# Row scatters of a group's last block: all at once, or two by two between other pieces of work

## The chip, the cores and the metric

The kernel runs on one core of one Trainium2 chip. The metric is the time of one execution on the device in microseconds (us). The core has five engines with an instruction queue each, and each queue runs in order: TensorE (PE, matrix products; PEld is its loading of weights), VectorE (DVE), ScalarE (ACT), GpSimd (POOL) and SyncE (SP, which issues most DMAs here). An engine waits for another one, or for a DMA, by a semaphore.

## The reference, cut to what matters

The input is x, 8 sequences of 1024 rows of 256 numbers, all in f32. An RWKV layer (a time mix with a scan along the sequence, then a channel mix with a hidden width of 1024) is followed by a layer of 32 routed experts, of which every row uses four. The change lies in how rows reach the experts.

```python
x = x + rwkv(layernorm(x))          # time mix, then channel mix
xn = layernorm(x)                   # 8192 rows of 256
gates = sigmoid(xn @ expert_sel.T)  # 32 experts
sel_val, sel_idx = top_k(gates, 4)
...
scores = relu(einsum('nd,edf->nef', xn, keys)) * gate_full[:, :, None]
out = x + einsum('nef,efv->nv', scores, values)   # 128 hidden units each
```

## The kernel before, in words

**Blocks and periods.** The rows are cut into 16 blocks of 512, two to a sequence. The main loop runs `period(i)` for i = 0 to 16. A period works on three blocks at once, by hand-written order: the channel mix of block i (`channel`, TensorE's products at L244 and L423), the time mix of block i + 1 (`mix_wk`, `mix_vr`, `mix_scan`, `mix_out`, `norm_c`), and the norm and routing of block i - 1 (`norm_d`, `apply_d`, `turn_d`, `gates_of`, `rows_of`, `scatter`). Between these pieces stand 15 calls of `advance()`. When a block's channel mix is over, its residual goes to DRAM (`acc<-x`, L445, on SyncE's queue); in the profile these stores mark the ends of the periods.

**Scatters.** Routing copies each row four times, to the regions of its experts in a DRAM buffer `xs` of its group. One scatter is an indirect DMA on GpSimd (L563), which sends 128 rows to 128 places; a block has 4 x 4 = 16. `scatter(i)` does not issue them: it puts 16 entries on the list `waiting`. `post(count)` issues the first `count` of the list, and `behind_others` keeps a scatter behind the GpSimd work that stands ahead of it in the program. GpSimd's other work in a period is the residual add of `norm_c` (L371, 2.4 us) and, in every second period, four copies of the scan's last column (`tail`, L320 and L321). The rows to scatter lie in a tile `x3` that has two buffers, so `apply_d` of block i + 2 (ScalarE, L363) writes where block i's rows were.

**Expert groups.** The blocks form two groups, `GROUPS = ((12, 6, 1.8, 4, 0.8), (4, 4, 1.0, 2, 1.0))`: blocks 0 to 11 and blocks 12 to 15. The numbers behind the size are: advances to wait before the table is made, tiles per advance, a pause, and sums per advance. A group's rows are worked in tiles of 256 rows of one expert (112 tiles for group 0, of which the last 16 are made of two halves with an expert each; 48 for group 1). `expert_group` is a stream that runs in the background: it makes the table that says which expert and which rows each tile has (`tile_table`, some 45 small steps on VectorE with three matrix products), then the tiles (`experts`), then the sums of the four results of each row (`combine`). A tile is fetched from `xs` on SyncE (L759), transposed on TensorE (`trx`, L794), multiplied by its expert's keys (`ph`, L806), passed through ScalarE (`hs`, L884), multiplied by the values (`po`, L822), copied by ScalarE (`yg`, L888) and scattered by GpSimd in two indirect DMAs to `ys` (L834). The three products of a tile lie two steps apart: in step n TensorE does `po` of tile n - 4, `ph` of tile n - 2 and `trx` of tile n. For group 0 the stream rests four resumptions between the first fetches and step 0 (the first `pause`).

**advance.** Each call issues one waiting scatter and lets each background stream do the work that its pace allows: a `yield` of 1.0 takes one advance, a `yield` of 1.8 a part of 1 / 1.8.

**Around the change.** Group 0's stream begins ahead of period 13 (`i == groups[g][-1] + 2`), group 1's after period 16; both times, `post(len(waiting))` first issues all waiting scatters. After that, `drain()` calls `advance()` until the streams are done. `blocks_over` then gives the tiles more buffers: `yg` takes turns with a tile of the channel mix, and fetches run five tiles ahead and not three. `x` and `out` are not touched by the change, nor is the number of any instruction that computes.

Of the kernel before, what the change touches and what calls it, by code (L numbers as in the profile page):

```python
# [34 lines left out]
def rwkv_then_routed_experts(  # L35
# [48 lines left out]
    group_of = {i: g for g, members in enumerate(groups) for i in members}  # L84
# [34 lines left out]
    def load_experts(part):  # L119
        es = slice(part * NE // 4, (part + 1) * NE // 4)  # L120
        tc.keep_in_program_order(nc.sync.dma_start(out=wexp[:, es], in_=w_exp[:, es]))
# [44 lines left out]
    def apart(kind, g, ins):  # L166

        key = f"{kind}_{g}"
        tc.declare_no_dep(ins.ins, group=key, reason="the rows are disjoint")
        tc.add_to_no_dep_group(key, ins.ins)  # L170

    def clear(g):


        zeros = p2.tile([P, DX], F32, tag="g", name=f"zeros_{g}")
        nc.gpsimd.memset(zeros, 0.0)
        nc.gpsimd.memset(zeros[:, D : D + 1], NOWHERE)
        front_rows = xs[g][: regions[g], :].rearrange("(e r) d -> e r d", e=NE)[:, :TS, :]
        fills = []
        for j in range(SJ):  # L180
            fills.append(
                nc.sync.dma_start(
                    out=front_rows[:, j * P : (j + 1) * P, :].rearrange("e p d -> p e d"),
                    in_=zeros[:, None, :].to_broadcast([P, NE, DX]),
                )
            )
            fills.append(
                nc.sync.dma_start(
                    out=xs[g][regions[g] + j * P : regions[g] + (j + 1) * P, :], in_=zeros
                )  # L190
            )
        for fill in fills:
            apart("scatter", g, fill)
# [345 lines left out]
    waiting = []  # L539
# [5 lines left out]
    def behind_others(s):  # L545

        own_names.add(s.ins.name)
        for other in reversed(nc.cur_bb.bb.instructions):
            if other.engine == ET.Pool and other.name not in own_names:
                tc.add_manual_dep(  # L550
                    s.ins,
                    other.name,
                    mybir.DependencyInfo(mybir.DependencyClass.NoSync, mybir.DependencyReason.DATA),
                    reason="the norms go first",
                )
                return

    def post(count):

        for i, t, k in waiting[:count]:  # L560
            m = mine[i]
            g = group_of[i]
            s = nc.gpsimd.indirect_dma_start(  # L563
                out=xs[g],
                out_offset=bass.IndirectOffsetOnAxis(ap=m["row"][:, t, k : k + 1], axis=0),
                in_=m["x3"][:, t, :],
                in_offset=None,
            )
            apart("scatter", g, s)
            behind_others(s)  # L570
        del waiting[:count]
# [381 lines left out]

    def advance():

        post(1)
        for entry in list(background):
            entry[1] += 1.0
            while entry[1] > 0.0:
                try:  # L960
                    entry[1] -= 1.0 / next(entry[0])
                except StopIteration:
                    background.remove(entry)
                    break

    def drain():
        while background:
            advance()

    def beside(stream):  # L970
        next(stream)
        background.append([stream, 0.0])
# [5 lines left out]
    def period(i):  # L978


        do(norm_d, i - 1)
        if i:
            do(mix_wk, i + 1, 0)
        advance()
        do(turn_c, i)
        if i:
            do(mix_vr, i + 1, 0)
        advance()
        do(apply_d, i - 1)
        do(fetch_block, i + 2)  # L990
        do(receptance, i)
        advance()
        do(channel, i, 0)
        if i:
            do(mix_scan, i + 1, 0)
        advance()
        if i:
            do(mix_wk, i + 1, 1)
        do(turn_d, i - 1)
        do(norm_a, i + 2)  # L1000
        advance()
        do(channel, i, 1)
        advance()
        if i:
            do(mix_vr, i + 1, 1)
        advance()
        do(channel, i, 2)
        do(mix_scan, i + 1, 1)
        advance()
        do(gates_of, i - 1)  # L1010
        do(channel, i, 3)
        do(norm_b, i + 2)
        advance()
        do(channel, i, 4)
        advance()
        do(mix_out, i + 1)
        do(norm_c, i + 1)
        advance()
        do(channel, i, 5)
        do(rows_of, i - 1)  # L1020
        do(scatter, i - 1)
        do(turn_b, i + 2)
        advance()
        do(channel, i, 6)
        advance()
        do(channel, i, 7)
        do(gates_by_row, i - 1)
        advance()
        do(apply_c, i + 1)
        do(channel_end, i)  # L1030
        advance()
# [21 lines left out]
    apply_c(0)  # L1053
    mix_scan(1, 0)

    done = set()

    def expert_group(g, wait, tiles, pause, sums):

        making = tile_table(g)  # L1060
        next(making)
        for _ in range(wait):
            yield 1.0
        for _ in making:
            pass

        while g and ("tiles", g - 1) not in done:
            yield 1.0
        for _ in experts(g, 0 if g else 4):
            yield tiles  # L1070
        done.add(("tiles", g))
        for _ in range(pause):
            yield 1.0
        while g and ("sums", g - 1) not in done:
            yield 1.0
        for _ in combine(g):
            yield sums
        done.add(("sums", g))

    for i in range(total_blocks + 1):  # L1080
        for g, (size, *pace) in enumerate(GROUPS):
            if i == groups[g][-1] + 2:
                post(len(waiting))
                beside(expert_group(g, *pace))
        period(i)
        if i + 1 < len(groups):
            clear(i + 1)
        elif 2 <= i < 6:
            load_experts(i - 2)
    blocks_over.append(True)  # L1090
    post(len(waiting))
    beside(expert_group(len(groups) - 1, *GROUPS[-1][1:]))
    drain()

# [44 lines left out]
```

## Time and profile before

| | us |
|---|---|
| median of 9 runs | 1501.15 (1497.11 to 1504.19) |
| the profiled execution | 1500.02 |
| its span in the profile | 1498.2 |
| granted TensorE clock, mean | 0.928 |
| GpSimd's row scatters (L563) | 256 of them, 255.1 busy |
| GpSimd's scatters of results (L834) | 320 of them, 320.3 busy |
| TensorE busy | 1278.1, 85% of the span |

In the lines shown further on, a line of a timeline gives the start (us from the span's beginning), the duration, the engine, the line of the kernel, the operation, what it writes and reads, its shape, how many such instructions are merged in the line, and in brackets how long the engine had been idle before it and what ended that. "remote" there means that no engine's instruction in the profile fits the moment of the release; "issue" means that the engine waited for nothing that the profile shows. A group's line ends with its busy time, the mean of one instruction in ns, and the idle time ahead of it. In the rows of 40 digits each digit is a slice of 37.5 us, in tenths of busy time.

### The profile page before, as it was taken

To read this page: it belongs to the slowest core of one execution; us is meant where nothing else is said; L and a number is where in the kernel's file an instruction comes from. 1 tells how busy PE (TensorE), PEld (TensorE's weight loads), DVE (VectorE), ACT (ScalarE), POOL (GpSimd) and SP (SyncE) were. 2 spreads that over 40 slices of the span, in tenths; PEclk is the share of its full clock that TensorE was granted. 3 is DMA by queue.
4 is the path that set the end of the run, shared out by engine and by line. 5 is a ranking of instruction groups with operands and counts; after the bars stand their busy time and mean duration, and the time that the engine had idled before them with its cause. 6 is when DMAs were issued, how large, how long until landed. Compare 5 with 4: busy or idle time off the path is not lost. (4 is left out here: it accounts for less than half of the span.)

```text
span 1498.2 us, 18501 instructions
## 1 busy us (share of the span) xinstructions
PE 1278.1 (85%) x5332; PEld 908.7 (61%) x5332; DVE 973.5 (65%) x3058; ACT 552.4 (37%) x1058; POOL 639.6 (43%) x643
## 2 busy tenths in 40 slices
PE   6999999999999998998958999998977748887720
PEld 2566667665665665665635767776765637666620
DVE  6777887886786786776837566543444524465697
ACT  3444444444444444443423343342322202434310
POOL 2003145134134134135070565665666665665640
PEclk9999999999999999999979999999988869989965
DMA  9901133133022021022031354454454543699898
GB/s 324 294 29 36 44 128 110 51 128 131 16 75 71 20 76 69 18 70 78 14 115 51 125 178 139 143 178 140 146 184 142 165 149 94 219 347 358 296 325 324
DMA packets 119412, 209.73 MB, mean 140 GB/s; under 512 B 17130, under 2 KB 77574, under 8 KB 118800
## 3 DMA queue, kind: packets, MB, share of 16 engines
q1 hardware_dynamic: 89616, 138.71, 29.0%
q0 software_dynamic: 27648, 68.23, 12.4%
q10 hardware_dynamic: 2048, 1.61, 0.3%
q8 instruction: 44, 0.72, 0.2%
q14 instruction: 56, 0.46, 0.1%
HBM read 105.68 MB, written 111.17 MB: 145 GB/s over the span
## 5 line engine op out<-in xcount | busy, mean ns | idle before, releaser
L834 POOL DMA_INDIRECT ys<-yg,to x320 | 320.3, 1001 | 226.1 <-ACT yg L888 116.9
L563 POOL DMA_INDIRECT xs<-x,row x256 | 255.1, 997 | 83.0 <-issue 67.1
L244 PE MATMUL pj_f<-xT,wkey 128*128 128x512 f32 x512 | 244.5, 600 | 1.7 <-ACT hs L884 1.2
L423 PE MATMUL cm<-wval,k 128*128 128x256 f32 x1024 | 240.9, 380 | 0.1
L822 PE MATMUL po<-wexp,hs 128*128 x640 | 185.3, 416 | 64.9 <-ACT hs L884 54.1
L423 PEld LDWEIGHTS cm<-wval,k 128*128 128x128 f32 x1024 | 194.8, 191 | 74.8 <-issue 50.1
L806 PE MATMUL ph<-xgT,key 128*128 128x256 f32 (+1 forms) x768 | 182.6, 371 | 23.2 <-DVE key L785 8.9
L878 DVE COPY xgT<-trx 128x512 f32<-128x512 f32 x112 | 77.0, 687 | 184.1 <-PE trx L794 70.8
L371 POOL TENSOR_TENSOR x<-x,xa 128x1024 f32<-128x1024 f32 x16 | 37.7, 2357 | 328.9 <-issue 317.2
L822 PEld LDWEIGHTS po<-wexp,hs 128*128 128x128 f32 x640 | 121.3, 208 | 87.9 <-ACT hs L884 59.3
L806 PEld LDWEIGHTS ph<-xgT,key 128*128 128x128 f32 x768 | 141.1, 208 | 47.6 <-DVE key L785 11.5
L884 ACT ACTIVATE hs<-ph 128x256 f32<-128x256 f32 x160 | 62.2, 389 | 283.5 <-PE trx L794 115.4
L415 ACT ACTIVATE k<-pj_f 128x512 f32<-128x512 f32 x128 | 76.5, 598 | 187.2 <-PE pj_f L244 179.4
L244 PEld LDWEIGHTS pj_f<-xT,wkey 128*128 128x128 f32 x512 | 93.3, 192 | 73.1 <-issue 67.7
L917 DVE SCALAR_TENSOR_TENSOR ac<-g,gate,ac 128x256 f32<-128x256 f32 x256 | 120.9, 484 | 22.2 <-DMA g<-ys 14.4
L794 PE MATMUL trx<-ident,xg 128*128 128x128 f32 x640 | 103.1, 287 | 12.2 <-ACT hs L884 9.1
L325 DVE RECIPROCAL rw<-rw 128x512 f32<-128x512 f32 x32 | 107.3, 3352 | 1.0
L794 PEld LDWEIGHTS trx<-ident,xg 128*128 128x128 f32 x640 | 84.6, 150 | 29.8 <-ACT hs L884 10.0
L785 DVE COPY key<-wexp 128x256 f32 x192 | 57.7, 308 | 58.6 <-remote 20.7
L888 ACT COPY yg<-po 128x512 f32<-128x512 f32 x160 | 93.8, 587 | 1.5 <-PE po L822 1.5
L321 POOL COPY tail<-ek 128x1 f32<-128x1 f32 x16 | 16.6, 1040 | 163.3 <-DVE ek L317 139.8
L397 PE MATMUL rec<-att,xT 128*128 128x256 f32 x256 | 71.5, 439 | 17.2 <-ACT xT L383 9.9
(162 smaller groups left out, 1764.6 us busy)
## 6 DMA issues: line engine op xcount, KB each, us to landing
xg<-xs SPq DMA_DIRECT2D x128, 264.0 KB
g<-ys SPq DMA_DIRECT2D x64, 512.0 KB
xs<-zeros SPq DMA_DIRECT2D x4, 4224.0 KB
xg<-xs SPq DMA_DIRECT2D x64, 132.0 KB
x<-in_x SPq DMA_DIRECT2D x16, 512.0 KB
acc<-x SPq DMA_DIRECT2D x16, 512.0 KB
wexp<-in_w_exp SPq DMA_DIRECT2D x4, 2048.0 KB
ac<-acc SPq DMA_DIRECT2D x16, 512.0 KB
```

The source lines that it names most:

```text
L244: nc.tensor.matmul(ps, w(c), rhs[:, c, :], start=(c == 0), stop=(c == KC - 1))
L325: inverse = nc.vector.reciprocal(rc, rc)
L415: nc.scalar.activation(k2, ps, AF.Relu)
L423: nc.tensor.matmul(m["cm"][t // 2][:, t % 2, :], k2[:, t * P : (t + 1) * P], wval[:, f, :], start=(f == 0 and t % 2 == 0), stop=(f == FC - 1),
L563: s = nc.gpsimd.indirect_dma_start(out=xs[g], out_offset=bass.IndirectOffsetOnAxis(ap=m["row"][:, t, k : k + 1], axis=0), in_=m["x3"][:, t ...
L794: nc.tensor.transpose(ps[:, c, j * P : (j + 1) * P], xg[:, j, c * P : (c + 1) * P], ident)
L806: nc.tensor.matmul(ps[:, cols], key[:, c * P : (c + 1) * P], xgT[:, c, cols], start=(c == 0), stop=(c == KC - 1),)
L822: nc.tensor.matmul(ps[:, j, :], hs[:, j * P : (j + 1) * P], wexp[:, bass.ds(e, 1), KC * P :], start=True, stop=True,)
L834: s = nc.gpsimd.indirect_dma_start(out=ys[g], out_offset=bass.IndirectOffsetOnAxis(ap=to[:, j : j + 1], axis=0), in_=yg[:, j, :], in_offse ...
L878: after(move(xgT, trx), signal)
L888: after(nc.scalar.copy(yg, po), signal)
L917: nc.vector.scalar_tensor_tensor(ac, gk, routed[i][:, t, k : k + 1], ac, ALU.mult, ALU.add)
```

## The change

`advance` issues two scatters where the first waiting one is of a group whose stream has begun, else one as before. The two calls of `post(len(waiting))` are gone, so the scatters that wait when a stream begins are issued two by two by the following advances. The stream makes its table as before, and then yields, an advance at a time, until none of its group's scatters waits; only then come its fetches and tiles.

```diff
     def advance():
 
-        post(1)
+        post(2 if waiting and group_of[waiting[0][0]] in begun else 1)
         for entry in list(background):
...
-    done = set()
+    done, begun = set(), set()
 
     def expert_group(g, wait, tiles, pause, sums):
 
+        begun.add(g)
         making = tile_table(g)
         next(making)
         for _ in range(wait):
             yield 1.0
         for _ in making:
             pass
+
+        while any(group_of[i] == g for i, _, _ in waiting):
+            yield 1.0
 
         while g and ("tiles", g - 1) not in done:
             yield 1.0
@@
     for i in range(total_blocks + 1):
         for g, (size, *pace) in enumerate(GROUPS):
             if i == groups[g][-1] + 2:
-                post(len(waiting))
                 beside(expert_group(g, *pace))
         period(i)
...
     blocks_over.append(True)
-    post(len(waiting))
     beside(expert_group(len(groups) - 1, *GROUPS[-1][1:]))
     drain()
```

## The prediction

> **What bounds the kernel now.** I read the page first, for the span and the slices; then the busy time by stage, cut where a block's residual is stored (SyncE's `acc<-x` at 645.82, 699.44, 761.48, 863.96, 980.56 and 1092.89 us); then GpSimd's and the other engines' timelines at the two places that the change touches.
>
> From the page:
>
> ```profile
> span 1498.2 us, 18501 instructions
> PE   6999999999999998998958999998977748887720
> POOL 2003145134134134135070565665666665665640
> L834 POOL DMA_INDIRECT ys<-yg,to x320 | 320.3, 1001 | 226.1 <-ACT yg L888 116.9
> L563 POOL DMA_INDIRECT xs<-x,row x256 | 255.1, 997 | 83.0 <-issue 67.1
> ```
>
> From its second slice to slice 28 TensorE is at 8 or 9 tenths but for one hole, slice 20 (749 to 787 us), just where GpSimd is busiest; later it is the less busy one. A scatter takes 1.0 us, and 1.27 from start to start.
>
> Stage by stage (length, busy time and instructions of each engine, granted clock, DMA):
>
> ```profile
> core 0: us, PE busy (x) PEld busy (x) DVE busy (x) ACT busy (x) POOL busy (x), PEclk, DMA share, GB/s
> 645.80:699.40 53.60, 53.11 (x206) 34.77 (x206) 42.23 (x124) 23.82 (x43) 20.84 (x22) 1.00 0.17 58
> 699.40:761.50 62.10, 56.62 (x209) 36.08 (x209) 42.81 (x131) 24.61 (x44) 18.02 (x17) 0.95 0.15 53
> 761.50:864.00 102.50, 82.74 (x344) 58.68 (x343) 57.18 (x223) 32.71 (x62) 42.92 (x43) 0.88 0.31 98
> 864.00:980.60 116.60, 113.59 (x533) 87.18 (x532) 72.15 (x234) 44.44 (x93) 74.41 (x73) 1.00 0.48 154
> 980.60:1092.90 112.30, 102.74 (x477) 81.08 (x477) 47.84 (x198) 39.52 (x85) 67.44 (x69) 0.94 0.49 152
> 1092.90:1201.70 108.80, 80.40 (x368) 64.64 (x366) 49.89 (x221) 26.51 (x62) 71.24 (x72) 0.86 0.53 168
> 1201.70:1230.30 28.60, 8.59 (x26) 6.45 (x27) 4.60 (x23) 1.96 (x6) 18.35 (x19) 0.62 0.40 134
> 1230.30:1289.40 59.10, 48.10 (x280) 42.45 (x279) 27.14 (x115) 17.12 (x40) 37.63 (x38) 0.90 0.36 106
> ```
>
> The rows are periods 11 to 16, then the drain up to group 0's last send. Period 11 is a block alone: 53.6 us, all TensorE. Period 14 holds a block and 28 tiles and is all TensorE: (116.6 - 53.6) / 28 = 2.25 us a tile. In the last row 19 tiles (38 sends) take 59.1 us, 3.11 each, with GpSimd issuing 1.28 us apart for 82% of it. Two rows do little: period 13, and the 28.6 us at 1201.7, with 8.6 us of TensorE.
>
> Period 13's start, on GpSimd:
>
> ```profile
> 746.04 2.35 POOL L371 TENSOR_TENSOR x<-x,xa 128x1024 f32<-128x1024 f32 x1 [39.51 <-issue]
> 748.55 0.99 POOL L563 DMA_INDIRECT xs<-x,row  x1 [0.15 <-issue]
> ...
> 783.20 0.96 POOL L563 DMA_INDIRECT xs<-x,row  x1 [0.30 <-issue]
> 791.01 1.10 POOL L321 COPY tail<-ek 128x1 f32<-128x1 f32 x1 [6.85 <-DVE rs_d L230]
> ```
>
> and on TensorE and ScalarE:
>
> ```profile
> 761.61 1.04 PE L237 MATMUL tr_c<-ident,xn 128*128 128x128 f32 x8
> 772.69 0.78 ACT L383 ACTIVATE xT<-tr_c,csb 128x512 f32<-128x512 f32 x1 [10.65 <-remote]
> 782.52 0.78 ACT L383 ACTIVATE xT<-tr_c,csb 128x512 f32<-128x512 f32 x1 [9.06 <-remote]
> ```
>
> The 23 held scatters and the 5 before them make one unbroken run of 28, 748.5 to 784.2. TensorE's transposes are over at 762.7, yet ScalarE copies them out only at 772.69 and 782.52, and "remote" says that no engine's work released it then. VectorE's table steps, 0.2 us each, stand one to two us apart. It ends as the run ends. Shorter cases agree: the run of 15 that ends at 706.5 holds ScalarE's same copy 7.1 us, in period 12 (62.1 us, 8.5 over period 11); period 11, whose runs are 8 at most, has no such wait. So I read a long run of scatters as delaying the signals between the other engines while it lasts.
>
> **The change, part by part.** A period has 15 calls of advance and a block 16 scatters, so the backlog grows by one a period: 23 wait when period 13 begins (7 of block 10, 16 of block 11), 15 when the drain begins.
>
> *1. Period 13 loses its stall.* In the built program's order GpSimd now has 11 scatters behind norm_c's add (748.5 to about 762.5, at 1.27), then two, six, two and four between the tail copies, then the add of block 14 and eight more. This is period 11's pattern (8, tail, 2, tail, 2) with longer runs. Of the 102.5 us, 53.6 is the block, about 22.5 ten tiles at 2.25, about 4.5 the front ends of four more (four transposes at 0.60, two products at 1.03, from the timeline); 21.9 is stall. At least none of it goes, at most all; I keep 3 for the runs of six and eight, since period 11's run of 8 cost nothing to see and period 12's run of 15 cost 8.5. Gain 18.9.
>
> *2. The tiles start later.* The table is still made at the sixth advance; the fetches now follow the twelfth. Four resumptions are pause, 1.8 go to an advance: before, 18 resumptions give 14 steps in period 13; now 8 give 4. In the built order ten fewer tiles are sent before the drain as well. Ten tiles leave a period where each costs 2.25 (gain 22.5) and join the drain, where each costs 3.11 (loss 31.1): net loss 8.6. Bounds of the drain's price: 2.25 if GpSimd kept out of the way, 3.89 at period 16's pace (108.8 / 28, its own 16 scatters in it); 3.11 is the row of the same stage. Periods 14 to 16 keep 27 steps each.
>
> *3. What the new wait holds.* The fetch waits on SyncE for group 0's last scatter. Period 11's add starts 39.2 us in (685.04), so here near 801 to 803; 2.4 us for it, three scatters (3.8), then landing: first fetch near 809, against 808.27 before. Its tile reached TensorE 3.4 us after the issue, so 812, about where the fourteenth advance stands. Behind it on SyncE stand three fetches and the store of block 13 (about 820): nothing late. ScalarE's norm of block 12 needs block 10's scatters landed, the last behind the first tail copy; period 11 has the same and waited 3.4 us with no harm. Cost taken as 0, at most 8 if TensorE stands until the fetch.
>
> *4. The drain's 15 scatters.* The 28.6 us hold the run of 15 and two tiles' sends: 28.6 - 2 x 3.11 = 22.4 us for the run. Posted in pairs they still cost GpSimd 15 x 1.27 = 19.1. Gain 3.3. Bounds: 11 gained if the pairs fit GpSimd's idle (3.11 - 2.56 = 0.55 us a tile over 14.4 tiles, 8 us); 19 lost if each of eight pairs brings one more restart of 2.35 us (the usual gap there until ScalarE's `yg`). Group 1's tiles wait for group 0's anyway, 31 tiles or 17 advances, so the eight for its scatters cost nothing; without that cover one advance is some 6 us. The 208.8 us behind keep their order.
>
> Sum: -18.9 - 22.5 + 31.1 + 0 - 3.3 = -13.6 us, from the profiled execution's 1500.02 (span 1498.2 and 1.8 around it) to 1486.4. The median of the nine, 1501.15, is 1.1 above that execution: 1487.5, said as 1488.
>
> The row that carries this is ScalarE's wait beside a scatter run. The Trainium skill (SBUF — State Buffer, "Who interferes with whom") says otherwise: only the port pair of VectorE and GpSimd contends, and TensorE and ScalarE never wait on anyone. By that rule the 21.9 us would not be the run's doing; by the row, 19.7 us of waits of a ScalarE copy lie inside it. The trace does not bear the rule out here, if the rule is meant for signals as well as ports. What it would make of the time is the second rival.
>
> **The rivals.**
> (a) *Short runs hold TensorE too.* Period 13 still has runs of 11, 8 and 8. If each held it as the run of 15 did (8.5), the period takes 53.6 + 4.5 + 25.5 = 83.6, the gain there is 18.9 in all, and the sum -18.9 + 31.1 - 3.3 = +8.9: 1510. It decides from a period 13 above about 75 us. For: in the drain ScalarE waits up to 5.7 us, "remote", beside runs of six sends. Against: period 11.
> (b) *The stall has another cause* (the table's chain on VectorE, the clock of 0.88). Then only the tiles move: +8.6, the run gains nothing: 1510. For: VectorE's table falls in the same 25 us. Against: the stall at 699, which has no table.
> (c) *It evens out*: ten tiles at 3.89 and 3 us of stall more: -13.6 + 7.8 + 3 = -2.8, about 1498 to 1502. For: GpSimd gets the pairs in the drain beside the moved tiles. Against: period 16 less its scatters, (108.8 - 16 x 1.27) / 28 = 3.16 a tile.
> (d) *It does not do what it says*: excluded by the built order, in which the pairs stand between the other pieces.
>
> **How the numbers follow.** Forecast 0.64 (own range 1474 to 1498), (a) 0.17, (b) 0.08, (c) 0.11. Under about 0.2%, 3 us, no change can be told. Faster: the forecast and a fifth of (c), 0.66; same: the most of (c), 0.09; slower: (a) and (b), 0.25. The range: down to 1472, the whole stall gone (-3), the pairs hidden (-7.7) and the moved tiles at 2.6 (-5); up to 1510 for (a) and (b).
>
> **What would show it.** Period 13 between stores: near 61 us (right), above 75 (rival a). ScalarE's 10.65 and 9.06 waits gone at its start (step 1); gone with no gain, rival (b). First fetch near 809 and four tiles transposed by the period's end (2, 3). From the drain's first pair to group 0's last send near 115 us, against 87.7 now (2, 4); over 130 makes the prediction wrong. The stretch behind near 209.

## The result, and the profile after

| | us |
|---|---|
| the changed kernel, median of 20 runs | 1488.46 (1480.22 to 1494.65) |
| the kernel before on the same chip, median of 62 | 1498.89 (1492.88 to 1506.85) |
| ratio | 0.9927, 95% interval 0.9914 to 0.994 |
| the profiled execution after | 1493.14, span 1491.4, granted clock 0.933 |

The change makes the kernel faster by 0.7%, some 10 us. From the page of the changed kernel, the lines that were shown of before:

```profile
span 1491.4 us, 18515 instructions
PE   6999999998998999999999999889777667778730
POOL 2002145134144044135054456656666665566640
L834 POOL DMA_INDIRECT ys<-yg,to x320 | 321.9, 1006 | 225.2 <-ACT yg L888 132.6
L563 POOL DMA_INDIRECT xs<-x,row x256 | 254.9, 996 | 80.5 <-issue 68.5
```

TensorE's hole in slice 20 is gone, and GpSimd's 7 there is a 5. The number and the cost of the scatters are the same. In exchange TensorE's thinner part, once the blocks are over, reads 7 7 7 6 6 7 7 7 from slice 28 on. Stage by stage, with the same columns and cuts as before (stores of the residual, the first pair of the drain at 1159.7, group 0's last send at 1277.8):

```profile
core 0: us, PE busy (x) PEld busy (x) DVE busy (x) ACT busy (x) POOL busy (x), PEclk, DMA share, GB/s
643.00:697.60 54.60, 54.11 (x209) 35.26 (x208) 43.24 (x126) 24.23 (x43) 20.89 (x22) 1.00 0.17 57
697.60:758.07 60.47, 56.85 (x209) 36.36 (x208) 42.79 (x129) 24.45 (x43) 17.76 (x18) 0.94 0.15 54
758.07:820.70 62.63, 55.89 (x218) 36.07 (x217) 42.61 (x169) 25.19 (x44) 28.64 (x28) 0.97 0.25 87
820.70:937.08 116.38, 113.40 (x532) 86.78 (x530) 70.96 (x235) 44.34 (x92) 66.03 (x66) 1.00 0.46 146
937.08:1044.88 107.80, 97.84 (x459) 78.62 (x460) 48.53 (x198) 36.60 (x79) 65.89 (x67) 0.94 0.50 156
1044.88:1159.70 114.82, 85.38 (x384) 68.03 (x383) 49.05 (x220) 28.72 (x67) 74.83 (x75) 0.86 0.52 166
1159.70:1277.80 118.10, 80.38 (x413) 67.61 (x412) 45.38 (x187) 25.75 (x59) 75.97 (x77) 0.85 0.41 127
1277.80:1491.40 213.60, 121.27 (x624) 102.95 (x624) 147.38 (x445) 63.78 (x143) 98.88 (x96) 0.79 0.92 321
```

Period 13 (758.07) takes 62.6 us where it took 102.5, and period 15 4.5 less. Period 16 and the drain together take 232.9 where they took 196.5. At the start of period 13, on GpSimd and on ScalarE (timeline; the columns are those of the timelines before):

```profile
742.62 2.35 POOL L371 TENSOR_TENSOR x<-x,xa 128x1024 f32<-128x1024 f32 x1 [37.98 <-issue]
745.13 0.98 POOL L563 DMA_INDIRECT xs<-x,row  x1 [0.16 <-issue]
...
758.03 0.96 POOL L563 DMA_INDIRECT xs<-x,row  x1 [0.30 <-issue]
```

```profile
760.83 0.60 ACT L293 ACTIVATE ek<-pj_w 128x512 f32<-128x512 f32 x1 [6.21 <-remote]
761.32 1.44 ACT L383 ACTIVATE xT<-tr_c,csb 128x512 f32<-128x512 f32 x2
```

The unbroken run is 11 scatters long and over at 759.0. ScalarE's two copies, which waited 10.65 and 9.06 us, now follow each other without a wait. The first fetch, on SyncE:

```profile
810.30 7.38 SPq L759 DMA_DIRECT2D xg<-xs  x4
```

It came at 810.3, and its tile reached TensorE at 813.41. Three tiles were transposed before the store at 820.70 that ends the period, and the fourth 0.4 us behind it.

Single executions differ by some us, so both kernels were profiled a second time, on one other chip (e11 and e12 below). Each stretch's change in us, after less before:

| stretch | predicted | first pair of profiles | second pair |
|---|---|---|---|
| ahead of period 13 | 0 | -3.4 | -4.0 |
| period 13 | -41.4 | -39.9 | -42.2 |
| period 14 | 0 | -0.2 | -2.3 |
| period 15 | 0 | -4.5 | -6.8 |
| period 16 and the drain | +27.8 | +36.4 | +37.8 |
| the stretch behind | 0 | +4.8 | -1.1 |
| sum | -13.6 | -6.8 | -18.6 |
| medians of timed runs | -13.6 | -10.4 | -12.9 |

(41.4 is the stall's 18.9 and ten tiles' 22.5; 27.8 is their 31.1 less the pairs' 3.3. In the second pair the drain is cut at the first gather of the sums.) The stretch ahead of period 13 holds nothing that the change touches until 745 us, and the one behind the drain differs by 4 us between the two profiles of the changed kernel alone (212.2 and 207.8 from the first gather); so the sums of single profiles lie on both sides of the medians.

Part of two rows is the same work, counted once as lost and once as gained. In the rows above period 15 has 459 of TensorE's products where it had 477, and period 16 has 384 where it had 368: a tile has twelve (four each of `trx`, `ph` and `po`), so a tile and more has slipped from one period into the next. In the second pair it is 463 for 481 and 385 for 368. Periods 15 and 16 together take 222.6 us for 221.2, and 222.0 for 222.5.

### The profile page after: what moved, and what is told of

Its sections match the earlier page's. It is cut to its first block, busy times and chain, and to the rows that moved or that the text cites. A ratio compares the mean times of both kernels' runs of the same rounds, so it can differ in the third digit from the quotient of the medians.

```text
span 1491.4 us, 18515 instructions
## 1 busy us (share of the span) xinstructions
PE 1278.9 (86%) x5332; PEld 908.8 (61%) x5332; DVE 974.4 (65%) x3058; ACT 553.0 (37%) x1058; POOL 640.2 (43%) x643
## 5 line engine op out<-in xcount | busy, mean ns | idle before, releaser
L822 PE MATMUL po<-wexp,hs 128*128 x640 | 190.0, 424 | 64.7 <-ACT hs L884 39.7
L794 PE MATMUL trx<-ident,xg 128*128 128x128 f32 x640 | 102.5, 285 | 28.1 <-ACT hs L884 24.7
L785 DVE COPY key<-wexp 128x256 f32 x192 | 61.1, 326 | 59.0 <-remote 17.3
L416 ACT ACTIVATE k<-k 128x512 f32<-128x512 f32 x128 | 80.7, 631 | 4.0
```

The lines of the kernel that those rows point to most:

```text
L416: nc.scalar.activation(k2, k2, AF.Square)
L794: nc.tensor.transpose(ps[:, c, j * P : (j + 1) * P], xg[:, j, c * P : (c + 1) * P], ident)
L822: nc.tensor.matmul(ps[:, j, :], hs[:, j * P : (j + 1) * P], wexp[:, bass.ds(e, 1), KC * P :], start=True, stop=True,)
```

## The experiments

Edits are shown against the kernel before or the changed kernel, as said. Ratios are to the kernel before on the same chip; e1 to e4 ran on one chip (1511.94 us before), e5 to e8 on a second (1516.27), e9 and e10 on a third, e11 and e12 on a fourth (1498.6).

### Which half of the change does it: e3 and e2

The changed kernel, with one of the two `post(len(waiting))` put back: e3 at group 0's start, so that only the drain has pairs; e2 ahead of the drain, so that only period 13 has them.

```diff
             if i == groups[g][-1] + 2:
+                post(len(waiting))          # e3
                 beside(expert_group(g, *pace))
...
     blocks_over.append(True)
+    post(len(waiting))                      # e2
     beside(expert_group(len(groups) - 1, *GROUPS[-1][1:]))
```

> The changed kernel, but the 23 scatters that wait when period 13 begins are issued at once, as before, and group 0's tiles start after the sixth advance; only the drain's 15 go in pairs. Theory as predicted: 3 us below the kernel before; period 13 as before, near 102 us. Rival (the pairs cost in the drain): 5 to 8 us above the kernel before.

> The changed kernel, but the 15 scatters that wait when the drain begins are issued at once, as before. Theory as predicted (pairs in the drain save 3.3 us): 3 us above the changed kernel, 7 us below the kernel before. Rival (the pairs cost in the drain, since period 16 and the drain together came out 36 us longer and not 28): 8 us below the changed kernel, 18 us below the kernel before.

e3 took 1512.06, ratio 1.0004 (0.9982 to 1.0026): no change. Its period 13 is 102.9 us and has the stall:

```profile
777.29 0.78 ACT L383 ACTIVATE xT<-tr_c,csb 128x512 f32<-128x512 f32 x1 [11.49 <-issue]
788.48 0.78 ACT L383 ACTIVATE xT<-tr_c,csb 128x512 f32<-128x512 f32 x1 [10.41 <-remote]
```

e2 took 1499.47, ratio 0.9927 (0.9901 to 0.9952): the whole gain of the change; period 13 is 60.0 us. So the gain comes with the pairs in period 13, and those in the drain are worth nothing that shows: by e3's interval they gain at most 2.7 us and cost at most 3.9. Both of what was expected of the drain's pairs, 3 us of gain and 5 to 8 us of cost, is outside that.

### The late tiles alone: e1

The kernel before, run of 28 and all, whose stream rests six advances between the table and the first fetch of group 0, about as long as the changed kernel's waits for its scatters.

```diff
         for _ in making:
             pass
+        for _ in range(0 if g else 6):
+            yield 1.0
```

> The kernel before (all scatters at once, twice), but group 0's stream rests six advances between its table and its first fetch, so its tiles start after the twelfth advance, as in the changed kernel. Theory (a long run of scatters stalls period 13): the stall stays, the tiles are only moved; period 13 near 80 us, ScalarE's copy of the transposes (L383) still waits some 10 and 9 us at its start, and the time is 8 to 9 us above the kernel before. Rival (the gain of the change comes from starting the tiles later, once the block is through): 8 to 12 us below the kernel before, as the changed kernel.

1518.21 us, ratio 1.005 (1.0021 to 1.0078). Stretches of e1, then those of e3, whose tiles start early, on the same chip (period 13, period 15, and period 16 with the drain up to the first gather):

```profile
765.93:847.67 81.74, 57.11 (x218) 36.57 (x217) 44.10 (x169) 25.29 (x44) 27.58 (x28) 0.87 0.20 66
963.81:1069.83 106.02, 96.50 (x463) 76.75 (x462) 49.80 (x197) 37.61 (x79) 66.14 (x67) 0.97 0.52 158
1069.83:1307.80 237.97, 164.17 (x796) 133.94 (x794) 95.58 (x405) 54.90 (x127) 150.80 (x152) 0.84 0.47 143
```

```profile
764.56:867.48 102.92, 82.11 (x344) 57.80 (x343) 57.01 (x224) 32.81 (x62) 42.66 (x43) 0.90 0.32 98
988.60:1100.78 112.18, 102.63 (x477) 80.69 (x477) 48.02 (x198) 39.19 (x85) 67.51 (x69) 0.94 0.50 150
1100.78:1301.34 200.56, 138.79 (x670) 115.34 (x668) 81.56 (x358) 44.93 (x104) 126.54 (x129) 0.86 0.47 142
```

Late tiles with the stall kept: period 13 gets 21.2 us shorter (ten tiles at 2.12), period 15 6.2, and period 16 with the drain 37.4 longer. Period 15 is shorter because it holds less: 463 products for 477, and TensorE is busy 6.1 us less. (Period 14, not shown, is 116.1 us for 121.1; it varies from 111 to 122 between the profiles here.) The stall is there: ScalarE's first copy waits 19.04 us in one piece. What the late tiles cost, and what leaves period 15, thus come from the order of the tiles and need no pairs. All told they cost 6.3 us by the medians (3.2 to 11.8 by the interval).

### The table, or the run: e4 and e5

e4: the kernel before, with the first part of the table, too, made only after the advances that the stream waits for, and so behind the run. e5: the kernel before, which also posts all that waits ahead of period 7, where there is no table and no expert tile.

```diff
-        next(making)                        # e4
         for _ in range(wait):
             yield 1.0
+        next(making)
         for _ in making:
             pass
...
     for i in range(total_blocks + 1):
+        if i == 7:                          # e5
+            post(len(waiting))
```

> The kernel before, but the whole of group 0's table is made at the sixth advance, so none of its steps on VectorE lies beside the run of 28 scatters. Theory (the run itself holds the other engines): ScalarE's copy of the transposes (L383) still waits some 10 and 9 us, period 13 stays above 98 us, the time within 5 us of the kernel before. Rival (the table's chain of small steps on VectorE makes the stall): the waits are gone, period 13 near 80 us, the time some 20 us below.

> The kernel before, but all waiting scatters (17) are also issued at once at the start of period 7, where no table is made and no tiles run; period 13's run falls from 28 to 22. Theory (a long run alone makes the stall): the run in front of period 7 has 22 scatters, lasts 28 us and reaches some 14 us into it; period 7 goes from 52.8 to 62 to 70 us and ScalarE's copy L383 waits 10 us or more there; period 13 falls from 102 to 92 to 97 us. Rival (the stall belongs to period 13's start of the expert group): period 7 stays at 53 us.

e4: 1521.31 us in one run, period 13 103.8 us. All but five of the table's small steps come at 804.8 us and later, behind the run (up to 785; the five are over at 756), and the waits are there without them (timeline, then the waits of the period: total, times, longest):

```profile
782.50 0.78 ACT L383 ACTIVATE xT<-tr_c,csb 128x512 f32<-128x512 f32 x1 [14.19 <-remote]
789.51 0.78 ACT L383 ACTIVATE xT<-tr_c,csb 128x512 f32<-128x512 f32 x1 [5.71 <-remote]
```

```profile
ACT xT L383 <- remote: 19.9, 2, 14.2
DVE ev L304 <- remote: 13.2, 1, 13.2
```

The time is 9 us above the median of before, where at most 5 was expected; single runs of before on that chip go from 1501 to 1519 us, so this one run can't tell. The chain is held rather than holding: its steps from L619 to L686 take 4.3 us here (804.8 to 809.1), with no run beside them, and 26.3 us in the kernel before (760.6 to 786.9).

e5: 1501.74 us in one run. An unbroken run of 22 scatters now stands at 407.2 to 435.2, and period 7 takes 68.7 us where its neighbours without a run take 53. Periods 7, 8 and 13:

```profile
420.50:489.15 68.65, 58.89 (x202) 36.88 (x201) 42.57 (x124) 24.93 (x44) 22.34 (x23) 0.90 0.15 50
489.15:542.32 53.17, 53.08 (x206) 34.86 (x205) 42.35 (x124) 24.29 (x44) 17.90 (x17) 1.00 0.17 59
764.64:857.17 92.53, 81.88 (x339) 57.44 (x340) 56.54 (x224) 32.66 (x62) 35.72 (x36) 0.91 0.31 97
```

```profile
437.14 0.78 ACT L383 ACTIVATE xT<-tr_c,csb 128x512 f32<-128x512 f32 x1 [12.76 <-remote]
```

The stall goes where the run goes, at the same copy, and period 13, whose run is shorter by what was posted early, is 10 us shorter. The table is not the cause. Nor is the granted clock: it falls with the stall (0.90 in period 7, 1.00 in period 8), and in the kernel before the copy waits 10 us although its transposes have ended. But the lower clock is a part of the price: TensorE is busy 58.9 us in period 7 for 202 products and 53.1 us in period 8 for 206.

### Breaking the other runs, and a version that beats both: e6, e7, e8

Periods 6, 8, 10 and 12 of the kernel before take some 60 us, and 7, 9 and 11 some 53. Only the even ones have a run of 15 ahead of them, since GpSimd's `tail` copies, which break the runs, are made in every second period. e6 (against before) makes them in every period; the added copies are read by nothing. e7 is the same on the changed kernel. e8 adds to e7 that two scatters also go whenever more than 16 wait, so that the backlog never grows to 23.

```diff
-        if n + 1 < NB:                      # e6, e7, e8
+        if tail is not None:
...
-        post(2 if waiting and group_of[waiting[0][0]] in begun else 1)   # e8
+        post(2 if waiting and (len(waiting) > 16 or group_of[waiting[0][0]] in begun) else 1)
```

> The kernel before, but the four copies of the scan's last column on GpSimd are made in every period and not in every second one (the added copies are read by nobody). Each waits for VectorE's scan and so breaks the runs of 15 scatters that lie ahead of periods 6, 8, 10 and 12. Theory: these periods fall from 60 to 62 us to about 53, 7 to 8 us each, 25 to 31 us in all below the kernel before; period 13 stays. Rival (runs of 15 are harmless and the longer periods have another cause): no change, or up to 8 us above for 16 more copies of 1 us on GpSimd.

> The changed kernel with the copies of the scan's last column in every period. Theory: 25 to 31 us below the changed kernel, 35 to 41 us below the kernel before: the two gains add, since they lie in different periods. Rival as in the run before: as the changed kernel.

> As the run before, and advance also issues two scatters while more than 16 wait, so about 12 and not 23 wait when period 13 begins: they are gone by the sixth advance, when the table is made, and group 0's tiles start as early as in the kernel before. Theory: no stall and no tiles moved to the drain: 5 to 12 us below the changed kernel with paced scatters. Rival (the tiles' start is worth nothing, as it only moves them): the same as that kernel, within 3 us.

| | us | ratio to before |
|---|---|---|
| e6, before with broken runs | 1484.0 | 0.9797 (0.9758 to 0.9836) |
| e7, after with broken runs | 1476.06 | 0.9745 (0.9704 to 0.9785) |
| e8, and a short list | 1458.52 | 0.9626 (0.9584 to 0.9667) |

In e6 periods 6 and 8 fall to 52.8 us and period 10 to 54.1; period 12 (61.0) does not, though it was expected to, and period 13 keeps its stall at 101.3. At period 12's start ScalarE's copy L383 waits only 1.4 us, but `apply_d` waits 6.2 us for row scatters to land, and the period's last 16.7 us lie beside the run of 28, which begins earlier here. The four periods are 22 us shorter than in the first profile of before; e6's median is 32.3 us below that of before on its chip, where 25 to 31 was expected and before was not profiled. e7 is 40.2 below it (35 to 41 expected), and e8 17.5 below e7 (5 to 12 expected).

In e8 the list is short when group 0's stream begins, so its tiles start early, and the longest run there is of 12, with a gap. e8's periods 12 and 13, and its period 16 with the drain:

```profile
677.81:730.41 52.60, 52.60 (x206) 34.67 (x205) 42.46 (x130) 24.13 (x44) 21.31 (x22) 1.00 0.18 60
730.41:814.81 84.40, 80.12 (x347) 57.43 (x346) 55.86 (x224) 32.43 (x62) 35.98 (x36) 0.96 0.35 108
1046.53:1244.65 198.12, 133.96 (x664) 110.26 (x662) 80.84 (x352) 45.28 (x105) 125.07 (x127) 0.86 0.46 141
```

With 14 tiles in it e8's period 13 is 84.4 us; the prediction's terms without a stall give 53.6 + 22.5 + 4.5 = 80.6. So the stall in the kernel before was 18 to 22 of the 102.5. Period 16 and the drain take 198.1 us with the tiles early and 238.2 in e7, where they are late (its period 13 is 60.9); but periods 14 and 15 are 113.2 and 108.4 us in e7, for 121.6 and 110.1 in e8. From period 14 to the first gather the late tiles cost 29.9 us, 3.0 for each of ten. (TensorE has nearly the same number of products in the two periods, 1002 and 999; why they are shorter is not shown.)

### Gaps in the run: e9 and e10

The kernel before, with GpSimd writing zeros to a scratch tile after every fourth scatter of a pile: in e9 one write of 128 x 1, in e10 six of 128 x 256. The question was whether GpSimd's being busy counts, or the scatters standing back to back.

```diff
             behind_others(s)
+            if count > 2 and nth % 4 == 3:
+                tc.add_manual_dep(
+                    nc.gpsimd.memset(pad, 0.0).ins,
+                    s.ins.name,
...
+                )
```

> The kernel before, with one memset of 128 x 1 on GpSimd (0.1 us) after every fourth scatter of the two piles issued at once. Theory (the signals pass only when GpSimd stops to wait, or works on something else for a time): a gap of 0.1 us changes nothing; ScalarE's copy L383 still waits some 20 us in all at the start of period 13, which stays near 102 us. Rival (any other instruction in the run lets the signals through): waits under 8 us each scatter group, period 13 near 85 to 90 us.

> The kernel before, with six memsets of 128 x 256 on GpSimd (some 0.3 us each, 1.9 us together) after every fourth scatter of the two piles. Theory: every gap of this length lets the other engines' signals through; the longest wait of ScalarE's copy L383 falls to about 5 us (four scatters), period 13 to 82 to 92 us, though GpSimd is busy 10 us longer. Rival (the scatters' number, or their transfers still under way, holds the signals, not the unbroken run): L383 waits as before, period 13 at 102 us or longer.

1376.71 and 1394.22 us in one run each. The kernel before, too, took only 1373.64 there (one run), 8 to 9% under what it took on the three other chips. So the gaps were not tested, since there was no hold to break: ahead of e9's first gap stands the same unbroken run of 15 in period 12 as before, and nobody waits for it. GpSimd's run and ScalarE's copy, in e9 (the added lines move the scatter to L564):

```profile
666.59 0.99 POOL L564 DMA_INDIRECT xs<-x,row  x1
...
684.61 0.96 POOL L564 DMA_INDIRECT xs<-x,row  x1 [0.30 <-issue]
```

```profile
680.20 0.78 ACT L383 ACTIVATE xT<-tr_c,csb 128x512 f32<-128x512 f32 x1 [1.50 <-PE tr_c L237]
```

and the same copy in the kernel before on the fourth chip (e11):

```profile
709.59 0.78 ACT L383 ACTIVATE xT<-tr_c,csb 128x512 f32<-128x512 f32 x1 [7.88 <-remote]
```

The run has the same length and the same pace, 15 scatters in 19 us. In e9 the copy is released by the transposes, as the program has it, while the run is still going on; period 12 takes 52.6 us, and in e11 60.8, where the copy waits 7.88. Period 13 of e9 is 80.9 us, with 14 tiles: the 80.6 of the prediction's terms without a stall; e10's, with the long gaps, is 95.1, with a wait of 11.0 us for a tile's fetch in it. In the lists of waits of e9 and e10 none is ended by "remote".

### Both kernels once more: e11 and e12

No edit. The question was whether the hold, and with it the gain, is there on a fourth chip.

> The kernel before, unchanged, for a profile beside e12 on one chip. Theory (a long unbroken run of GpSimd's scatters holds the releases of the engines beside it, and how much of it differs from chip to chip): period 13 of 100 to 104 us and waits of 10 us or more at L383 where the total is near 1500; where the total is near 1374, period 13 of 78 to 84 us, no such wait, and the even periods 6, 8, 10 and 12 at 53 us in place of 60. Rival (the program has one behaviour, and the 1374 came from the clock alone): period 13 of 95 us or more and even periods of 58 to 60 us at any total.

> The changed kernel, unchanged, timed against the kernel before on the chip of e11. Theory: where the kernel before has its stall, 0.993 of its time as measured. Where it has none, only the ten moved tiles and the drain's pairs count: period 13 goes from about 80 to about 60 us, the drain takes ten tiles more at 3.1 to 4.0 us each against 2.25 in a period, and the kernel is 8 to 18 us slower, 1.006 to 1.013 of the time before. Rival (the gain has nothing to do with the stall): 0.993 on any chip.

It is: before 1498.6 us (11 runs), after 1485.72, ratio 0.9916 (0.9893 to 0.9938). e11's period 13 takes 102.5 us, and ScalarE's two copies wait 10.63 and 9.05 us, as in the first profile to 0.02 us.

In e12 the period takes 60.4 us, and of the two copies the first waits 2.4 us, for TensorE. The expectation for a chip without the stall, 8 to 18 us of loss, was not put to the test: the changed kernel was not run on the chip of e9.

## Why the prediction was right, step by step

The mechanism is as predicted, and of the four steps one, the drain's pairs, was wrong in size. That 1488 was predicted and 1488.46 measured is in part luck: the gain came out at 10.4 us and not 13.6, and the kernel before at 1498.89 us in 62 runs and not 1501.15 in nine, and the two differences offset each other. Without the pairs' 3.3 us the sum would have been -10.3.

**Step 1, the stall: right.** Period 13 near 61 us was predicted, and it took 62.6 and 60.4. That the run is the cause, which was read off one wait and a shorter case, is now shown from three sides: undoing the pairs there brings the stall back (e3), moving the table away leaves it (e4), and a run put elsewhere takes the stall with it (e5). Its size, 21.9, is 18 to 22 by e8 and e9.

**Step 2, the tiles: right, though the drain's own row looks worse.** Ten tiles in a period were worth 21.2 us in e1 (22.5 predicted), and the net loss of 8.6 us was 6.3 there. In the four pairs of runs with late and early tiles period 16 and the drain are 36.4, 37.8, 37.4 and 40.1 us longer, and not 31.1. But in the first three pairs 14 to 18 products, a tile and more, have left period 15 for period 16, and period 15 is shorter by 4.5 to 6.8 us. From the drain's first scatter on, the tiles can be read alone: 62 sends are made there and not 42, just the ten tiles (us from the first of the 15 scatters to the first gather of the sums):

| | the 15 at once | in pairs |
|---|---|---|
| tiles early | 90.7 (before), 89.5 (e11) | 90.6 (e3) |
| tiles late | 120.2 (e1), 122.4 (e2) | 119.5 (after), 120.9 (e12) |

The late tiles cost 29 to 33 us in it, 2.9 to 3.3 each, around the 3.11 of the prediction. What was not foreseen is that a tile would slip from period 15 into period 16: 27 steps in each were predicted, and period 16 is longer by 6 to 8 us. Why the cut between them falls elsewhere in the order of the steps was not tried.

**Step 3, the fetch's wait: right.** Predicted near 809 and 812, it came at 810.3 and 813.4, with three tiles in the period and the fourth just behind it. Nothing was late behind it.

**Step 4, the drain's pairs: nothing, and not 3.3 us of gain.** e3 bounds the gain at 2.7, and e2, without the pairs in the drain, has the ratio of the change, 0.9927. The table above says the same row by row: 89.5 to 90.7 at once and 90.6 in pairs, 120.2 and 122.4 at once and 119.5 and 120.9 in pairs. The sum had taken the run's 22.4 us as paid for the run alone, and 19.1 as the price of its pairs. The waits that "remote" ends are not less in all, only shorter each: ScalarE's for `hs`, from the drain's first scatter to group 0's last send, before (87.7 us, with one wait of 23.0) and after (118.1 us, with ten tiles more; total, times, longest):

```profile
ACT hs L884 <- remote: 47.2, 6, 23.0
ACT hs L884 <- remote: 50.1, 9, 9.1
```

Where the 3.3 us went is not shown beyond that. The stretch took 118.1 us where 115 was predicted and 130 was the limit; the difference is about the pairs' 3.3.

**The rivals.** (a), short runs hold as much, falls with period 13 at 60 to 63 us. A run of 11 still shows, as ScalarE's wait of 6.21 us at L293 above, and it is the only wait of the period that "remote" ends; in e12 there is none. (b), another cause, falls with e4 and e5, its clock included. Its rule, the Trainium skill's (SBUF — State Buffer, "Who interferes with whom") that TensorE and ScalarE never wait on anyone, read as one on signals too, does not agree with the traces of three chips, in which a ScalarE copy stands 7.1 to 19.0 us beside a run; it agrees with e9's on the third chip, where the copy waits 1.5 us for its transposes. (c), it evens out, falls too: the ten tiles cost 2.9 to 3.3 each and not its 3.89, and the medians moved by 10.4 and 12.9 us.

**What stays open.** By what the runs hold the other engines. A release that comes long after the releasing instruction's end is what "remote" stands for here, and the traces' lists of semaphore updates show it: the update that lets the copy at 772.69 us go is recorded 0.02 us ahead of the copy, 10 us behind the end of its transposes, and in e9, at the copy at 680.20, each transpose's update is recorded 0.01 us behind the transpose's end. The Trainium skill (Perfetto Trace Analysis, "Summary: the profiler window per engine type") lists the passing on of semaphore updates as hidden from the profile for these engines, which fits; where on its way an update is late, no run here shows.

And why one chip has none of it: there the kernel before was timed once, and only e9 and e10 were profiled. Those two traces differ from all others in one more thing. They have nearly every update on record (797 for the 796 that TensorE's instructions make in e9, and 14,672 for the DMAs' 14,736), and the others lack some beside GpSimd's transfers: in the kernel before 717 of TensorE's and 5,407 of the DMAs' are recorded, though of the compute engines' none is missing ahead of the first transfer. Whether the recording of updates has a part in the hold, or only suffers from the same cause, and so whether it is the chip that differs, no run here separates.

## What to carry to other kernels

A queue that is full of small indirect transfers can cost more through what it holds up than through its own time: look for waits of other engines that end when the run ends, and test it by moving the run. Rather than pacing a backlog where it hurts, keep it from growing (e8: two scatters as soon as more than 16 wait, and something else between them in every period), for then no consumer has to start later; with both, e8 was worth 3.7% on its chip, five times the change. And before a stretch's growth is read as the price of moved work, count the instructions in it and in its neighbours: of the 36 to 38 us that period 16 and the drain grew by in three pairs of profiles, the ten tiles are about 31.

## What was not expected of the hardware

- The hold is a matter of length. Periods are 53 us with runs of 8; with a run of 15 they are longer by 7.4 us (60.2 less 52.8), with 22 by 15.9 (e5), with 28 by 18 to 22. That is, as an estimate from these three, 0.9 to 1.1 us for each scatter beyond the eighth, a little under the 1.27 us at which they are issued.
- It was absent on one chip: there the same run of 15 held nothing, in the same program part, and the kernel before took 1373.64 us in place of about 1500 to 1516. More than the stalls is missing there: period 15 takes 93.9 us in e9 and 112.9 in e11, the stretch from its end to the first gather 166.2 (with gaps in its last pile of scatters) and 199.1, and what is behind that 191.7 and 208.9. That these are the same hold, beside the tiles' scatters, is not shown. A gain that rests on such a hold is a gain where the hold is.
